# Layer 1 attention: three of four heads with held weights, one with moving weights

## The chip, the cores and the metric

The kernel runs on one core of one Trainium2 chip. The metric is the device time of one execution in microseconds (us); less is better. A core has five engines that run side by side and meet only at semaphores: TensorE (PE in the profile, with its loads of stationary operands as PEld), VectorE (DVE), ScalarE (ACT), GpSimd (POOL) and SyncE (SP). [...]

## The reference, cut to what matters

Two layers follow each other, each with a residual sum and a layer norm at its end. There are 16 graphs (batches) of 1024 nodes with 256 features and a 0/1 adjacency matrix for each. Layer 0 is graph attention with 4 heads of 64. The change is in the attention of layer 1, which has 8 heads of 32:

```python
normed = layer_norm(x, gamma1, beta1)
qkv = normed.reshape(b_, n_, H, HD).transpose(0, 2, 1, 3)
scale = 1.0 / jnp.sqrt(jnp.asarray(HD, dtype=x.dtype))
scores = jnp.einsum('bhqd,bhkd->bhqk', qkv, qkv) * scale
mask = adj_matrix[:, None, :, :] > 0
masked = jnp.where(mask, scores, -jnp.inf)
attn = jax.nn.softmax(masked, axis=-1)
out = jnp.einsum('bhqk,bhkd->bhqd', attn, qkv)
out = out.transpose(0, 2, 1, 3).reshape(b_, n_, d_)
x = x + out
y = layer_norm(x, gamma2, beta2)
mlp = jax.nn.gelu(y @ W1 + b1, approximate=False) @ W2 + b2
return x + mlp
```

Everything is float32. Queries, keys and values are the same tensor, so a block of weights comes out with keys on the partitions and queries along the free axis, which is what the product with the values needs.

## The kernel before

**Two layers at once.** While one batch is in layer 1, the next one or two are in layer 0. Both layers are generators (`layer0`, `layer1`) that emit a piece of work and yield. A planner at the end of `fast_path` picks which one emits next. It goes by two things: how much of its work a layer has done (fixed numbers handed over at each `yield`, 2.5 for a step of attention 1), held against a target course, and whether one layer would have to wait over 0.3 us longer than the other by the planner's own cost model (class `Pace`, which adds up a cost for each instruction on each engine). So instructions have a fixed order on each engine, written down when the program is built. Smaller follow-up work (dividing by sums, norms, transposes) is put into `chains`; `advance` emits the next part of a chain when the model says that its inputs are there.

**Attention 1** (`attention1`) goes over 32 steps in a batch: two halves of 512 queries (`n`), two groups of four heads (`quad`), eight blocks of 128 keys (`jb`); 512 steps in the whole run. A step has these parts:

- `exponentials`: four matmuls, one for each head, with 32 rows each on four row tiles of the array; then four ACT exponentials of 128x512 out of four PSUM banks (ring `ps`, four buffers, so all four banks are used by every step);
- `masked`, emitted one step later: two DVE multiplications of 128x1024 by the 0/1 mask, each over two heads;
- `products`, emitted three steps later (`LAG = 3`): weights times values, summed in PSUM over the eight blocks of keys.

**The two forms of product.** In both, the array is cut into four column tiles of 32, at output partitions 0, 32, 64 and 96. In the *moved* form the values (128x32) are held and the 512 weights of a head move past them; a second matmul with `unit` (a column of ones and 31 of zeros) gives the sums of the weights. Heads 0 and 1 go this way: four matmuls, one on each tile, with values of head 0, values of head 1, sums of head 0, sums of head 1. In the *held* form 32 queries' weights (128x32) are held and the 33 columns of values (the last is 1, so the sum comes with them) move. Heads 2 and 3 go this way: 2 heads x 4 blocks of queries x 4 tiles = 32 matmuls. The profile shows every float32 matmul as two loads and two matmuls, so a step has 8 of the moved form and 64 of the held form.

**Out of PSUM.** `moved` (512 columns) and `held` (264 columns) take the two buffers of the ring `po` and are used for the eight blocks of keys of a quad. Then `heads_out` runs, 64 times in the run: ACT copies `moved` to SBUF (`oT`, name `oT1`); DVE takes the reciprocal of the sums in `held` and multiplies; TensorE transposes `oT` with four 128x128 transposes into a bank `pt`; DVE divides again out of `pt`. The next quad can write to the two buffers only after the copy and the first division have read them. After the second quad `finish1` makes the residual and the norm, and `mlp` follows when all 32 steps are done.

In the profile every line is L61, the helper that records the instruction for the planner; groups are told apart by the names of tiles: `po<-p,v` and `po<-p,unit` are moved products, `po<-v,p` held ones, `ps<-nT` the logits of attention 1, `acc<-v,p` the products of layer 0, other `acc` lines layer 0's preparation and transposes, `ranges` and `o` the reciprocals and divisions of `heads_out`.

## Time and profile before

| | us |
|---|---|
| median of three runs | 3437.51 |
| lowest and highest run | 3434.63, 3438.09 |
| profiled execution, span from the first to the last instruction (the time that the profile gives for it) | 3453.7 |
| TensorE matmuls busy in the span | 3312.8 (96%) |
| DVE busy | 2981.3 (86%) |
| ACT busy | 1935.6 (56%) |
| mean granted TensorE clock | 0.980 of full |
| moved products, busy | 552.9 (values), 552.7 (sums), side by side |
| held products, busy | 391.4 |

The profiled execution is 16.2 us, 0.5%, above the median. Spans and waits in the text are from it. "Busy" is the time in which at least one instruction of a group is under way; the matmuls of a group overlap, so the mean duration of one (197 ns for a held one) says little, and the distance from one start to the next is what a matmul takes from the path. A batch takes some 210 us, the first half of it attention 1, the second half its MLP, both interleaved with layer 0 of a later batch.

### The profile page before, as it was taken

To read this page: it belongs to the slowest core of one execution; us is meant where nothing else is said; L and a number is where in the kernel's file an instruction comes from. 1 tells how busy PE (TensorE), PEld (TensorE's weight loads), DVE (VectorE), ACT (ScalarE), POOL (GpSimd) and SP (SyncE) were. 2 spreads that over 40 slices of the span, in tenths; PEclk is the share of its full clock that TensorE was granted. 3 is DMA by queue.
4 is the path that set the end of the run, shared out by engine and by line. 5 is a ranking of instruction groups with operands and counts; after the bars stand their busy time and mean duration, and the time that the engine had idled before them with its cause. 6 is when DMAs were issued, how large, how long until landed. Compare 5 with 4: busy or idle time off the path is not lost.

```text
span 3453.7 us, 141035 instructions
## 1 busy us (share of the span) xinstructions
PE 3312.8 (96%) x64161; PEld 2252.1 (65%) x64161; DVE 2981.3 (86%) x5262; ACT 1935.6 (56%) x4192; POOL 418.6 (12%) x424
## 2 busy tenths in 40 slices
PE   5899999999999999999999999999999999999998
PEld 4558576675856758576585766757667585775846
DVE  5898898988979898898988989889898898989883
ACT  2563846547375573746637466473654737556373
POOL 1102011010110101101020110101101011010200
PEclk9899999999999999999999999999999999999999
DMA  5211202011020111202112020120201102010000
GB/s 135 51 22 40 44 27 57 15 44 40 28 59 21 42 34 34 56 19 59 22 38 46 24 57 19 41 43 26 59 15 46 38 28 62 18 44 23 23 6 15
DMA packets 95728, 131.30 MB, mean 38 GB/s; under 512 B 10385, under 2 KB 61585, under 8 KB 95121
## 3 DMA queue, kind: packets, MB, share of 16 engines
q1 hardware_dynamic: 75104, 87.58, 8.2%
q0 software_dynamic: 18432, 33.56, 6.6%
q8 instruction: 504, 8.26, 1.0%
q10 hardware_dynamic: 1584, 1.05, 0.1%
q14 instruction: 104, 0.84, 0.1%
HBM read 138.68 MB, written 17.04 MB: 45 GB/s over the span
## 4 chain that ended last, share of the span: by engine, by line
PE 72%; DVE 20%; ACT 5%; issue 2%; DMA 1%; POOL 0%; SPq 0%; POOLq 0%; ACTq 0%; DVEq 0%
PE po L61 28%; PE ps L61 24%; PE acc L61 20%; DVE p L61 15%; ACT p L61 2%; DVE o L61 1%; DVE x L61 1%; ACT sq L61 1%; DVE st L61 1%; DVE z L61 1%; ACT mask L61 1%; ACT hb L61 1%; DVE v L61 0%; ACT z L61 0%; DVE hb L61 0%
## 5 line engine op out<-in xcount | busy, mean ns | idle before, releaser
L61 ACT ACTIVATE p<-ps 128x512 f32<-128x512 f32 x2006 | 1042.2, 616 | 384.1 <-PE ps L61 341.5
L61 DVE TENSOR_TENSOR p<-p,mask 128x1024 f32<-128x1024 f32 x1024 | 1186.6, 1217 | 6.8 <-ACT p L61 6.8
L61 DVE SCALAR_TENSOR_TENSOR p<-cb,dinv,mask 128x512 f32<-128x512 f32 x1024 | 711.0, 744 | 0.1
L61 ACT ACTIVATE hid<-ps,b_sb 128x256 f32<-128x256 f32 x512 | 242.0, 473 | 795.0 <-PE ps L61 794.7
L61 PE MATMUL ps<-nT 32*128 32x512 f32 x4012 | 676.3, 655 | 0.0
L61 PEld LDWEIGHTS po<-v,p 128*32 128x32 f32 x32768 | 396.1, 110 | 333.2 <-issue 288.5
L61 PE MATMUL acc<-v,p 128*64 128x65 f32 x16384 | 562.2, 226 | 31.0 <-DVE p L61 14.3
L61 PEld LDWEIGHTS acc<-v,p 128*64 128x64 f32 x16384 | 515.2, 140 | 112.9 <-issue 59.0
L61 PE MATMUL po<-p,v 128*32 128x512 f32 x2048 | 552.9, 615 | 0.0
L61 PE MATMUL po<-p,unit 128*32 128x512 f32 x2048 | 552.7, 615 | 0.0
L61 PE MATMUL ps<-yT,w_sb 128*128 128x256 f32 x2048 | 489.8, 385 | 0.0
L61 PE MATMUL po<-w_sb,hid 128*128 128x256 f32 x2048 | 474.6, 384 | 0.0
L61 PEld LDWEIGHTS po<-w_sb,hid 128*128 128x128 f32 x2048 | 381.7, 190 | 54.5
L61 PEld LDWEIGHTS ps<-yT,w_sb 128*128 128x128 f32 x2048 | 375.5, 190 | 51.5
L61 PE MATMUL po<-v,p 128*32 128x33 f32 x32768 | 391.4, 199 | 12.4 <-issue 8.5
L61 PEld LDWEIGHTS po<-p,v 128*32 128x32 f32 x2048 | 78.5, 109 | 332.9 <-issue 174.7
L61 PEld LDWEIGHTS ps<-nT 32*128 32x128 f32 x4012 | 220.1, 186 | 98.0 <-issue 41.3
L61 POOL TENSOR_TENSOR r<-v,mhalf 128x1 f32<-128x1 f32 (+1 forms) x192 | 157.6, 831 | 705.7 <-DVE v L61 623.8
L61 DVE TENSOR_TENSOR z<-acc,bias_r 128x256 f32<-128x256 f32 x128 | 54.1, 423 | 181.7 <-ACT hb L61 181.4
L61 PE MATMUL acc<-w0e,xT 128*128 128x264 f32 x512 | 154.1, 425 | 37.2 <-DVE z L61 22.9
L61 POOL DMA_DIRECT2D ak<-in_adj_dram x128 | 69.7, 545 | 971.5 <-PE acc L61 959.0
L61 POOL TENSOR_TENSOR r<-v1s,mhalf 128x4 f32<-128x4 f32 x32 | 61.5, 1922 | 981.1 <-DVE v1s L61 981.1
(111 smaller groups left out, 2818.5 us busy)
## 6 DMA issues: line engine op xcount, KB each, us to landing
ak<-in_adj_dram POOLq DMA_DIRECT2D x128, 256.0 KB, 3.9
cb<-esr SPq DMA_DIRECT2D x64, 512.0 KB
xk<-in_x_dram SPq DMA_DIRECT2D x64, 256.0 KB
xl<-in_x_dram SPq DMA_DIRECT2D x32, 512.0 KB
out_dram<-z SPq DMA_DIRECT2D x128, 128.0 KB
w_sb<-in_L_gnn_W_dram SPq DMA_DIRECT2D x2, 1024.0 KB
esr<-rows SPq DMA_DIRECT2D x64, 4.0 KB
v<-in_L_gnn_a_src_dram SPq DMA_DIRECT2D x2, 320.0 KB
```

The source lines that it names most:

```text
L61: return method(*args, **kwargs)
```

## The change

Of the four heads of a quad, head 0 alone has its weights moving. Its 512 queries are cut into two sides of 256, and the four column tiles take values of side 0, sums of side 0, values of side 1, sums of side 1: still four matmuls, of 256 columns each in place of 512. Heads 1, 2 and 3 have their weights held: 48 matmuls in place of 32. The moved ones still come first, then the held ones, head by head; head 1 takes its weights from the first pair's tile, heads 2 and 3 from the second's.

`moved` has 256 columns in place of 512, `held` 396 in place of 264. In `heads_out` the copy is 128x256, there are two transposes in place of four, the first division covers three heads (12 reciprocals and 384 products to a partition in place of 8 and 256), and the second covers one head in two parts, one for each side (2 reciprocals and 64 products each, in place of one with 8 and 256). The numbers handed to the planner at each yield and its course are not touched; its cost model sees the new instructions.

```diff
--- before.py
+++ after.py
@@ -218,6 +218,7 @@
     PAIR = 2
     GB = 2
     QUAD = 4
+    SIDE = HALF // 2
     NEAR0 = math.sqrt(0.5 - 2.0**-10)
     NEAR1 = math.sqrt(0.5 + 2.0**-10)
     SCALE1 = 1.0 / math.sqrt(HD)
@@ -761,22 +762,26 @@
 
         def products(quad, jb, ps, moved, held):
             values = half(jb // BPH)[1][:, jb % BPH, :, :]
-            for e in range(PAIR):
-                hd = quad * QUAD + e
-                for at, v in ((e, values[:, hd, 0:HD]), (PAIR + e, unit)):
+
+            for side in range(PAIR):
+                for i, v in enumerate((values[:, quad * QUAD, 0:HD], unit)):
+                    at = (side * PAIR + i) * Q
                     nc.tensor.matmul(
-                        moved[at * Q : (at + 1) * Q, :], v, ps[0][:, e, :], start=jb == 0, stop=jb == NB - 1
+                        moved[at : at + Q, :],
+                        v,
+                        ps[0][:, 0, side * SIDE : (side + 1) * SIDE],
+                        start=jb == 0,
+                        stop=jb == NB - 1,
                     )
-            for e in range(PAIR):
-                hd = quad * QUAD + PAIR + e
+            for e in range(1, QUAD):
                 for q in range(BPH):
                     for at in range(0, P, Q):
                         nc.tensor.matmul(
-                            held[at : at + Q, q, e, :],
-                            ps[1][:, e, q * P + at : q * P + at + Q],
-                            values[:, hd, :],
-                            start=jb == 0 and e == 0 and q == 0,
-                            stop=jb == NB - 1 and e == PAIR - 1 and q == BPH - 1,
+                            held[at : at + Q, q, e - 1, :],
+                            ps[e // PAIR][:, e % PAIR, q * P + at : q * P + at + Q],
+                            values[:, quad * QUAD + e, :],
+                            start=jb == 0 and e == 1 and q == 0,
+                            stop=jb == NB - 1 and e == QUAD - 1 and q == BPH - 1,
                         )
 
         LAG = 3
@@ -800,8 +805,8 @@
                 continue
             n, quad, jb = steps[i - LAG]
             if jb == 0:
-                moved = ps_o.tile([P, HALF], F32, name="po")
-                held = ps_o.tile([P, BPH, PAIR, HD + 1], F32, name="po")
+                moved = ps_o.tile([P, SIDE], F32, name="po")
+                held = ps_o.tile([P, BPH, QUAD - 1, HD + 1], F32, name="po")
             products(quad, jb, ready.pop(i - LAG), moved, held)
             if jb == NB - 1:
                 if quad == 0:
@@ -814,28 +819,34 @@
 
     def heads_out(n, quad, moved, held, o, rinv):
 
-        oT = two.tile([P, HALF], F32, name="oT1")
+        oT = two.tile([P, SIDE], F32, name="oT1")
         nc.scalar.copy(oT, moved)
         of_heads = o.rearrange("p k (h e) -> p k h e", e=HD)
         rinv = rinv[:, n * BPH : (n + 1) * BPH, :]
 
-        def divide(first, sums, src):
-            heads = slice(quad * QUAD + first, quad * QUAD + first + PAIR)
-            nc.vector.reciprocal(rinv[:, :, heads], sums)
+        yield "vector", held
+        heads = slice(quad * QUAD + 1, (quad + 1) * QUAD)
+        nc.vector.reciprocal(rinv[:, :, heads], held[:, :, :, HD])
+        nc.vector.tensor_mul(
+            of_heads[:, :, heads, :],
+            held[:, :, :, 0:HD],
+            rinv[:, :, heads][:, :, :, None].to_broadcast([P, BPH, QUAD - 1, HD]),
+        )
+        yield "tensor", oT, side_ready
+        pt = side_bank([P, SIDE // P, P])
+        for c in range(SIDE // P):
+            nc.tensor.transpose(pt[:, c, :], oT[:, c * P : (c + 1) * P], ident)
+        yield "vector", pt
+        hd = quad * QUAD
+        for side in range(PAIR):
+            mine = slice(side * SIDE // P, (side + 1) * SIDE // P)
+            sums = pt[:, :, (side * PAIR + 1) * Q]
+            nc.vector.reciprocal(rinv[:, mine, hd], sums)
             nc.vector.tensor_mul(
-                of_heads[:, :, heads, :], src, rinv[:, :, heads][:, :, :, None].to_broadcast([P, BPH, PAIR, HD])
+                of_heads[:, mine, hd, :],
+                pt[:, :, side * PAIR * Q : side * PAIR * Q + HD],
+                rinv[:, mine, hd][:, :, None].to_broadcast([P, SIDE // P, HD]),
             )
-
-        yield "vector", held
-        divide(PAIR, held[:, :, :, HD], held[:, :, :, 0:HD])
-        yield "tensor", oT, side_ready
-        pt = side_bank([P, BPH, QUAD, Q])
-        for q in range(BPH):
-            nc.tensor.transpose(
-                pt[:, q, :, :].rearrange("p e z -> p (e z)"), oT[:, q * P : (q + 1) * P], ident
-            )
-        yield "vector", pt
-        divide(0, pt[:, :, PAIR:, 0], pt[:, :, 0:PAIR, :])
 
     def finish1(o, x1, yT, heads):
```

## The prediction

> **What bounds the kernel now.** I read the page's busy times first, then the chain of waits, then the timeline of a few attention steps, then the stretches of one batch.

> ```profile
> span 3453.7 us, 141035 instructions
> PE 3312.8 (96%) x64161; PEld 2252.1 (65%) x64161; DVE 2981.3 (86%) x5262; ACT 1935.6 (56%) x4192; POOL 418.6 (12%) x424
> ...
> PE 72%; DVE 20%; ACT 5%; issue 2%; DMA 1%; POOL 0%; SPq 0%; POOLq 0%; ACTq 0%; DVEq 0%
> PE po L61 28%; PE ps L61 24%; PE acc L61 20%; DVE p L61 15%; ACT p L61 2%; DVE o L61 1%; DVE x L61 1%; ACT sq L61 1%; DVE st L61 1%; DVE z L61 1%; ACT mask L61 1%; ACT hb L61 1%; DVE v L61 0%; ACT z L61 0%; DVE hb L61 0%
> ```

> TensorE sets 72% of the end, but a fifth of the chain is DVE's, nearly all of it the mask multiplications. They take turns inside one batch, as the stretches of the batch from 1610 us show (busy time of PE, PEld, DVE, ACT, POOL; clock; DMA):

> ```profile
> 1625.00:1640.00 15.00, 14.92 (x369) 7.95 (x356) 11.30 (x15) 12.50 (x31) 0.53 (x1) 1.00 0.48 122
> 1640.00:1655.00 15.00, 15.00 (x356) 7.72 (x355) 12.56 (x15) 11.82 (x26) 1.06 (x2) 1.00 0.20 39
> ...
> 1685.00:1700.00 15.00, 14.74 (x446) 8.06 (x440) 14.93 (x19) 10.45 (x21) 0.00 (x0) 1.00 0.01 3
> 1700.00:1715.00 15.00, 15.00 (x478) 8.53 (x474) 14.93 (x18) 6.26 (x13) 0.00 (x0) 1.00 0.01 3
> ```

> In the first half of attention 1 DVE has 2.4 to 3.7 us in 15 to spare; in the last 45 us none. The chain of waits there says the same: TensorE step by step, then one run of DVE.

> ```profile
> 1623.61 1.56 PE po L61 x69
> 1625.17 1.09 PE acc L61 x4
> 1626.25 1.07 PE ps L61 x8
> 1627.33 1.56 PE po L61 x69
> ...
> 1697.91 11.72 DVE p L61 x12
> ```

> The products' price is in the timeline (start, duration), in two steps that follow each other without a change of array shape between:

> ```profile
> 1708.59 0.62 PE L61 MATMUL po<-p,v 128*32 128x512 f32 x1
> ...
> 1709.05 0.59 PE L61 MATMUL po<-p,v 128*32 128x512 f32 x1
> ...
> 1709.47 0.73 PE L61 MATMUL po<-v,p 128*32 128x33 f32 x63
> 1710.01 0.60 PE L61 MATMUL po<-p,v 128*32 128x512 f32 x1
> ...
> 1710.87 0.76 PE L61 MATMUL po<-v,p 128*32 128x33 f32 x64
> 1711.56 0.63 PE L61 MATMUL acc<-v,p 128*64 128x65 f32 x14
> ```

> Start to start, the moved products take 0.88 us in two passes (0.46 and 0.42), the 64 held ones 0.54 (8.4 ns each) or 0.68 where the array's shape changes after them. A step's products are 1.56 us, as in the chain.

> **The change, part by part.**

> *Moved products.* The same eight instructions pass 256 columns in place of 512. Column time halves: of 0.883 us, 0.854 is two passes of 0.427, so -0.427 us a step. Bounds: 0 if a pass has a floor, -0.44 if the start halves too. I take -0.427, because 256 columns on the whole array (po<-w_sb,hid) go by in 3.65/16 = 0.228 us a pass, against 0.427 for 512.

> *Held products.* 32 instructions more (16 matmuls of two passes): 32 x 8.4 ns = +0.268 us a step. Bounds: 32 x 8.4 below, and above 32 x 30.7 ns = 0.98 (layer 0's held products, 2.949 us for 96). I take 8.4: same tile, same columns, and 64 in a row show no slowing.

> Net -0.159 us a step, -81.4 us over 512 steps if every step were on the path.

> [...]

> *How much is on the path.* From the chain of waits, window by window over the run, 292 runs of products (19 hold two steps', so 311 of 512 steps) lie on it with most of their time. What a step on the chain gives back depends on the logits' four banks. After a short step the fourth logit waits for the fourth exponential of the step before:

> ```profile
> 1703.18 1.77 PE L61 MATMUL ps<-nT 32*128 32x512 f32 x8
> 1703.83 0.29 PEld L61 LDWEIGHTS ps<-nT 32*128 32x128 f32 x2 [0.20 <-ACT p L61]
> ```

> The step from logits at 1700.55 to logits at 1703.18 took 2.63 us, and these logits 1.70 start to start instead of 1.07. From logits to exponentials 1.16 us and four exponentials 2.06 make a loop of 3.22 us; a step shorter than that hands its gain to a longer wait in the next. Steps on the chain by length: 147 over 3.374 us give 0.159 each, 23.4 us; 18 between 3.215 and 3.374 give what they exceed the loop by, 2.4; 75 below give nothing, and 11.9 us stay out. 44 steps' products at the tails, after the batch's last logits, give 7.0. In the last batch, where no layer 0 is left and six banks take turns, the chain's 30 steps give 4.8. Sum -37.6 us.

> *Two transposes fewer* (four took 0.585 into acc, 0.49 into ps; 0.27 for two): 36 of 64 sets are on the chain, -9.7 us. *The copy to oT* falls from 0.60 to 0.41 (COPY hb<-acc, 128x256, 410 ns): -0.19 at 18 places, -3.5. Elsewhere it stands ahead of the next exponentials on ACT, which has 44% free.

> *Divisions.* Reciprocal to product takes 0.235 us, product to the next instruction 0.342. Three heads: 8 to 12 elements adds 0.025 (177 ns for 4, 202 for 8) and 256 to 384 adds 0.13 (424 ns for 256, 684 for 512), +0.155. Two sides: twice about 0.20 + 0.15 in place of 0.577, +0.12. So +0.275 for each heads_out, 17.6 us in all. [...] 48 of 128 divisions are on the chain: +6.6 us.

> *Held products alone on the chain* (17 places, where the moved ones were already past): 17 x 0.268 = +4.6 us. No DMA is issued in a changed step. *Clock:* after PE had idled 2.6 us, at 3314 us, a pass took 0.61 in place of 0.42; no wait that grows here comes near that, so I take nothing for it (above: as many such places more, 3 us each).

> Sum: -37.6 - 9.7 - 3.5 + 6.6 + 4.6 = -39.6 us. It is a ceiling of sorts: the chain names only the last releaser, and others stood close behind. In six of the batches DVE's run starts some 15 steps in, in the others five steps later, so the two engines are nearly level there. Bounds are 0 (all absorbed) and -39.6; I take 60%, as DVE has a fifth of its time free in the stretches where most of the gain is made: -24 us. On the median, 3437.5 - 23.5 = 3414 us; in the profiled execution 3430.

> **The rivals.**

> *Absorbed.* DVE or the exponentials set every step, and PE just waits longer. For: 75 chain steps already at the loop, DVE full for 45 us a batch. Against: 147 long steps with no stall. 3437 us, or 3431 to 3444.

> *The order falls worse (slower).* The planner's model sees cheaper products too, and what it takes as late decides which layer emits next. Place: two attention steps with no layer 0 work between. The run has 94 such bare steps before the last batch; the one above took 2.63 us, and the next logits stood 0.63 longer. After the change it would be 2.47 us, and 3.215 - 2.47 = 0.745 is lost at each. A fifth of them (DVE's share of the chain) would cost nothing, so 40 more bare steps, two and a half a batch, use up the 24 us; 72 more cost 72 x 0.8 x 0.745 = 43 us: 3457. Against: a step hands the planner the same amount of work done as before.

> *Held products slow down in longer runs (slower).* If the added 32 cost twice the row, 16.8 ns (an estimate between 8.4 and 30.7), a step loses 0.11 us instead of gaining: 311 x 0.11 = +34, with the -9.7, -3.5 and +6.6 above 3465 us. The break-even is 0.427/32 = 13.3 ns for each added one. Against: every run of 64 goes at 8.4.

> *Everything kept.* All 81 us, the transposes' 128 x 0.135 = 17, less the divisions' 18: 3357 us, if the steps on DVE's runs gained as well. Against: DVE busy 14.93 of 15 there.

> **How the numbers follow.** Forecast (3390 to 3430) 0.50; everything kept 0.08; absorbed 0.14; order worse 0.21; held slower 0.07. Faster by over 0.2% (7 us, about what a measurement here can tell from none): 0.58; within: 0.14; slower: 0.28. For 8 in 10 I leave out the deep part of "kept" (0.06) and the dear ends of the two slower ones (0.13): 3380 to 3466; the forecast's own range is 3390 to 3430.

> **What would show it.** Moved products at 0.46 us and 96 held ones in 0.80 (0.94 with a change of shape) confirm the prices. More time in fourth-logit waits on ACT and in PE's waits for DVE p, by about 12 us and up, shows where the lost part went. DVE's busy time should rise by some 18 us, PE's fall by 40 to 90. I am wrong if a held matmul takes 10 ns or more, if bare steps grow well beyond 94, or if the chain turns to DVE for more than 30%.

## The result and the profile after

The changed kernel takes 3596.45 us (median of four runs, 3585.14 to 3599.10) against 3437.80 us before: 1.0442 times as long, with a 95% interval of 1.0416 to 1.0467 (the ratios here are those on record; the quotient of the two medians is 1.0461). By the medians it is 158.7 us slower where 23.5 us less was forecast, and it lies far outside the range of 3380 to 3466.

The page of the changed kernel gives the same views as before: span, busy times, one group of products, the instruction queue.

```profile
span 3594.6 us, 173690 instructions
PE 3299.6 (92%) x80417; PEld 2428.2 (68%) x80417; DVE 2999.4 (83%) x5390; ACT 1920.0 (53%) x4192; POOL 414.6 (12%) x424
q8 instruction: 631, 10.34, 1.2%
L61 PE MATMUL po<-v,p 128*32 128x33 f32 x49152 | 578.1, 199 | 165.0 <-issue 155.5
```

The last line's second field is the idle time of TensorE just before the group, and what ended it. The same two lines of the kernel before, which the prediction does not use:

```profile
q8 instruction: 504, 8.26, 1.0%
L61 PE MATMUL po<-v,p 128*32 128x33 f32 x32768 | 391.4, 199 | 12.4 <-issue 8.5 <-DVE o L61 3.3
```

TensorE's share fell from 96% to 92% of a longer span. It did not get more work (busy 3312.8 before, 3299.6 after). It stands idle in front of held products for 165.0 us where it stood 12.4, and nearly all of that is "issue": no semaphore, engine or transfer that the profile shows released it. The chain of waits of the changed kernel reaches back only to 3066 us, over the last 15% of the span, so it is no help here.

The timeline of TensorE in the changed kernel (start, duration; in brackets the idle time before) shows what the idle time looks like:

```profile
1919.89 0.88 PE L61 MATMUL po<-v,p 128*32 128x33 f32 x80
1920.94 0.33 PE L61 MATMUL po<-v,p 128*32 128x33 f32 x16 [0.17 <-issue]
1921.20 1.16 PE L61 MATMUL acc<-w0e,xT 128*128 128x264 f32 x4
1922.29 1.14 PE L61 MATMUL ps<-nT 32*128 32x512 f32 x8
1923.36 0.44 PE L61 MATMUL acc<-ident,oT 128*128 128x128 f32 x2
1923.73 0.40 PE L61 MATMUL po<-p,v 128*32 128x256 f32 x1
...
1923.97 0.38 PE L61 MATMUL po<-p,v 128*32 128x256 f32 x1
...
1924.19 0.95 PE L61 MATMUL po<-v,p 128*32 128x33 f32 x89
1926.72 0.27 PE L61 MATMUL po<-v,p 128*32 128x33 f32 x7 [1.59 <-issue]
1926.91 0.71 PE L61 MATMUL ps<-nT 32*128 32x512 f32 x4
```

The moved products cost what was forecast: first pass at 1923.73, second at 1923.97, held ones from 1924.19, so 0.46 us. But a run of 96 held ones stops in the middle: after 80 in one step, after 89 in the next. Between the two stops lie 16 held matmuls, 4 of layer 0, 8 logits, 2 transposes, 8 moved, 89 held: 127 matmuls, each with its load, so 254 instructions and two waits on semaphores, 256 in all.

With that the step's arithmetic is another one. A bare attention step before has 80 matmuls, 160 instructions, in 2.63 us: 256 in 4.2 us. After the change it has 112, 224 instructions, in 2.47 us: 256 in 2.8 us, which the loop stretches to 3.5. With a unit of layer 0's products (32 matmuls in 1.08 us) it is 4.2 before and 3.2 after.

### The profile page after: what moved, and what is told of

Read it like the earlier page. It is cut to its first block, busy times and chain, and to the rows that moved or that the text cites. A ratio compares the mean times of both kernels' runs of the same rounds, so it can differ in the third digit from the quotient of the medians.

```text
span 3594.6 us, 173690 instructions
## 1 busy us (share of the span) xinstructions
PE 3299.6 (92%) x80417; PEld 2428.2 (68%) x80417; DVE 2999.4 (83%) x5390; ACT 1920.0 (53%) x4192; POOL 414.6 (12%) x424
## 5 line engine op out<-in xcount | busy, mean ns | idle before, releaser
L61 ACT ACTIVATE p<-ps 128x512 f32<-128x512 f32 x2006 | 1042.4, 615 | 436.5 <-PE ps L61 393.6
L61 DVE TENSOR_TENSOR p<-p,mask 128x1024 f32<-128x1024 f32 x1024 | 1188.2, 1218 | 20.1 <-ACT p L61 19.4
L61 PEld LDWEIGHTS po<-v,p 128*32 128x32 f32 x49152 | 561.5, 111 | 278.2 <-issue 192.5
L61 PE MATMUL po<-v,p 128*32 128x33 f32 x49152 | 578.1, 199 | 165.0 <-issue 155.5
L61 DVE SCALAR_TENSOR_TENSOR p<-cb,dinv,mask 128x512 f32<-128x512 f32 x1024 | 709.7, 744 | 0.0
L61 PE MATMUL ps<-nT 32*128 32x512 f32 x4012 | 699.0, 665 | 2.2 <-issue 2.2
L61 ACT ACTIVATE hid<-ps,b_sb 128x256 f32<-128x256 f32 x512 | 239.1, 473 | 844.7 <-PE ps L61 844.4
L61 PE MATMUL acc<-v,p 128*64 128x65 f32 x16384 | 567.9, 227 | 35.1 <-issue 10.4
L61 PEld LDWEIGHTS acc<-v,p 128*64 128x64 f32 x16384 | 520.1, 141 | 117.2 <-issue 60.6
L61 PE MATMUL ps<-yT,w_sb 128*128 128x256 f32 x2048 | 484.6, 386 | 1.5 <-issue 1.5
L61 PE MATMUL po<-w_sb,hid 128*128 128x256 f32 x2048 | 473.0, 383 | 0.0
L61 PEld LDWEIGHTS ps<-yT,w_sb 128*128 128x128 f32 x2048 | 381.9, 191 | 55.8 <-issue 2.1
L61 PEld LDWEIGHTS po<-w_sb,hid 128*128 128x128 f32 x2048 | 381.8, 190 | 53.4
L61 PE MATMUL po<-p,unit 128*32 128x256 f32 x2048 | 332.3, 399 | 1.2 <-issue 1.2
L61 PE MATMUL po<-p,v 128*32 128x256 f32 x2048 | 331.9, 399 | 0.1
L61 PEld LDWEIGHTS po<-p,v 128*32 128x32 f32 x2048 | 78.8, 109 | 345.6 <-issue 199.0
L61 PEld LDWEIGHTS ps<-nT 32*128 32x128 f32 x4012 | 230.1, 189 | 109.6 <-issue 44.2
L61 POOL TENSOR_TENSOR r<-v,mhalf 128x1 f32<-128x1 f32 (+1 forms) x192 | 153.6, 810 | 688.1 <-DVE v L61 605.3
L61 DVE TENSOR_TENSOR z<-acc,bias_r 128x256 f32<-128x256 f32 x128 | 54.2, 423 | 202.0 <-ACT hb L61 199.9
L61 PE MATMUL acc<-w0e,xT 128*128 128x264 f32 x512 | 157.0, 432 | 36.7 <-DVE z L61 22.9
L61 POOL TENSOR_TENSOR r<-v1s,mhalf 128x4 f32<-128x4 f32 x32 | 61.5, 1923 | 1091.3 <-DVE v1s L61 1091.3
L61 POOL DMA_DIRECT2D ak<-in_adj_dram x128 | 69.7, 545 | 1002.3 <-PE acc L61 988.8
```

Of the source, the lines that this page charges most:

```text
L61: return method(*args, **kwargs)
```

## Experiments

Two theories besides that of the instructions were open: that the planner, which saw cheaper products, had put the work into a worse order, and that a held matmul is dearer in runs of 96. All ratios are to the kernel before, run alongside on the same chip (medians 3450.51 us in the first four experiments, 3448.91 in the last two).

### The changed work in the old order

```diff
+            for e in range(PAIR):
+                for v in (values[:, quad * QUAD + e, 0:HD], unit):
+                    nc.enter("tensor", "matmul", (Told(moved, Q, HALF), v, ps[0][:, e, :]), {})
+            for _ in range(PAIR * BPH * P // Q):
+                nc.enter("tensor", "matmul", (Told(held, Q, HD + 1), ps[1][:, 0, 0:Q], values[:, 0, :]), {})
+            nc.deaf = True
             for side in range(PAIR):
...
+            nc.deaf = False
```

`nc.enter` books an instruction with the planner without issuing it; while `deaf` is set, what is issued is not booked. `heads_out` is told the old copy, transposes and divisions in the same way.

> The changed kernel's instructions in exactly the order of the kernel before: the planner is told before's matmuls, copies and divisions while the changed ones are issued. Instruction theory (TensorE's instructions come in 16 KB packets of 256, and 256 of them never take less than about 3.4 us; the 96 held products of a step empty the packet faster, and 202 us of stalls inside held runs are the loss): as slow as the changed kernel, 3570 to 3620 us, stalls inside held runs 170 to 230 us. Order theory (the planner placed the work worse once it saw cheaper products; bare steps rose from 94 to 108): the loss goes, 3400 to 3440 us.

3626.00 us, 1.0520 times (1.0501 to 1.0538). The held runs' distances over 0.06 us come to 223.4 us. In the old order the changed work is slower by 175.5 us, in its own by 158.7: the planner's new order is not the loss.

### The old work in the new order

The mirror: the products and `heads_out` of before, while the planner is told the changed ones.

```diff
+            for _ in range(PAIR):
+                for v in (values[:, quad * QUAD, 0:HD], unit):
+                    nc.enter("tensor", "matmul", (Told(moved, Q, SIDE), v, ps[0][:, 0, 0:SIDE]), {})
...
+            nc.deaf = True
             for e in range(PAIR):
                 hd = quad * QUAD + e
...
```

> The mirror of the run in the old order: the instructions of the kernel before in exactly the changed kernel's order (the planner is told the changed ones). Instruction theory: as fast as before but for 14 more bare steps at about 0.6 us, 3430 to 3465 us, stalls inside held runs under 30 us. Order theory: about 3570 to 3600 us.

3455.23 us, 1.0015 times (0.9999 to 1.0031); 8.8 us in held runs. The two groups of held products, first of the changed work in the old order, then of the old work in the new one (L64 is the same helper, three lines further down):

```profile
L64 PE MATMUL po<-v,p 128*32 128x33 f32 x49152 | 583.1, 199 | 179.9 <-issue 172.0
```

```profile
L64 PE MATMUL po<-v,p 128*32 128x33 f32 x32768 | 390.5, 198 | 8.2 <-issue 4.6
```

The idle time goes with the instructions and not with the order. For the old work the order is worth 0.15%, 0.31% at the interval's end.

### One head's held products left out

```diff
             for e in range(1, QUAD):
+                nc.mute = e == QUAD - 1 and jb > 0
                 for q in range(BPH):
                     for at in range(0, P, Q):
                         nc.tensor.matmul(
                             held[at : at + Q, q, e - 1, :],
-                            ps[e // PAIR][:, e % PAIR, q * P + at : q * P + at + Q],
+                            ones if e == QUAD - 1 else ps[e // PAIR][:, e % PAIR, q * P + at : q * P + at + Q],
...
```

`mute` books the matmul and does not issue it. The planner sees the constant in place of the last head's weights, so a few steps come in another order than in the changed kernel.

> The changed kernel in its own order, but the held products of the quad's last head are left out in seven of eight key blocks (in the first block a constant stands in for its weights), so a step has 64 held instructions as before and TensorE has 14 of 512 x 0.268 us less. Instruction theory: the 202 us of stalls fall under 30 and about 70 us of work on the path go as well, 3300 to 3390 us. Order theory, or a higher price of each held matmul: only the work goes, 120 us at most, 3470 to 3540 us.

3406.28 us, 0.9877 times (0.9854 to 0.9900): 44 us faster than before, where the changed kernel is 159 slower. Of these 203 us the work that was left out accounts for 120 at 8.4 ns a matmul; the stops in held runs fell from 203.5 us to 58.0. Against a dearer matmul this run alone says little, as the work left out would then be worth more than 120 us. The changed kernel itself settles that: of 483 runs of 96 held matmuls that nothing interrupts, 258 have no stop inside, and these go at 8.6 ns a matmul in the median.

The run missed the instruction theory's 3300 to 3390 as well. 58.0 us were left in held runs where under 30 were expected: 44.9 at packet boundaries, nearly all the rest waits for DVE's masks. Its page has 34.7 us of "issue" in front of held products, against 155.5 in the changed kernel:

```profile
L64 PE MATMUL po<-v,p 128*32 128x33 f32 x32768 | 406.0, 199 | 67.3 <-issue 34.7
```

That stops remain at all fits the numbers: the moved products had become shorter and an undisturbed bare step of 160 instructions now takes 2.2 us, 256 in 3.5, just at the loop.

### 64 queries held at a time

```diff
             for e in range(1, QUAD):
                 for q in range(BPH):
-                    for at in range(0, P, Q):
+                    for at in range(0, P, TILE):
                         nc.tensor.matmul(
-                            held[at : at + Q, q, e - 1, :],
-                            ps[e // PAIR][:, e % PAIR, q * P + at : q * P + at + Q],
+                            held[at : at + TILE, q, e - 1, :],
+                            ps[e // PAIR][:, e % PAIR, q * P + at : q * P + at + TILE],
...
```

> The changed kernel with the weights held 64 queries at a time on two column tiles, in place of 32 on four: 48 held instructions in a step for the same arithmetic. Instruction theory: stalls inside held runs under 15 us; if each costs about 15.6 ns (half of layer 0's 30.7 ns for 65 columns) 3370 to 3430 us; if the load of 64 columns bounds each at 27 to 31 ns, a step's held products take 1.3 to 1.5 us and the time is 3520 to 3650 us, still without stalls. Order theory: 3570 us or more, with held runs at 0.75 us.

3650.88 us, 1.0588 times (1.0569 to 1.0607): the dearer of the two branches. From the page of this kernel:

```profile
span 3650.8 us, 124523 instructions
PE 3535.5 (97%) x55841; PEld 2586.1 (71%) x55841; DVE 2999.5 (82%) x5390; ACT 1924.4 (53%) x4192; POOL 418.7 (11%) x424
q8 instruction: 439, 7.19, 0.8%
L61 PE MATMUL po<-v,p 128*64 128x33 f32 x24576 | 829.3, 226 | 0.0
```

With fewer instructions the idle time in front of held products is 0.0 and TensorE is back at 97%: the stalls are gone, with the same three heads held and as many bare steps as in the changed kernel (108). The time is lost elsewhere: 48 held matmuls take 1.42 us, 29.6 ns each, where the array's shape stays the same after them, though they move 33 columns where layer 0's move 65 for 30.7; and the moved products ahead of them take 0.57 us in place of 0.46. So the time goes with the 64 columns that are held and not with the columns that move; whether their load sets it was not shown.

### The price of 256 instructions by itself

```diff
     while chains:
         run(chains[0])
+    for i in range(2048):
+        if i % 16 == 0:
+            spare = ps_s.tile([P, BPH, HD + 1], F32, name="ps")
+        at, q = i % 4 * Q, i // 4 % BPH
+        nc.nc.tensor.matmul(spare[at : at + Q, q, :], unit, g1_r[:, 0 : HD + 1], start=True, stop=True)
```

> The kernel before with a run of 2048 extra held matmuls (4096 instructions pairs of load and matmul, 128x32 by 33 columns, on the four column tiles in turn, of constants, never read) after the last of TensorE's work; the planner is not told of them. It measures the disputed price by itself. 8192 instructions are 32 packets of 256. Instruction theory: 32 x 3.4 to 3.5 us = 109 to 112 us on the time, and the run stalls once in 256 instructions. A price for each matmul alone (8.4 ns for each pass): 4096 x 8.4 ns = 34 us.

3565.52 us, 116.6 us more than before (1.0338 times, 1.0317 to 1.0359): 3.6 us for each packet, where the matmuls' own 8.4 ns would have made 34 us of it. The timeline of TensorE at the end of this kernel:

```profile
3430.12 2.65 PE L1048 MATMUL ps<-g_r,unit 128*32 128x33 f32 x268
3434.97 1.38 PE L1048 MATMUL ps<-g_r,unit 128*32 128x33 f32 x128 [2.20 <-issue]
3438.99 1.99 PE L1048 MATMUL ps<-g_r,unit 128*32 128x33 f32 x128 [2.65 <-issue]
3442.47 1.99 PE L1048 MATMUL ps<-g_r,unit 128*32 128x33 f32 x128 [1.49 <-issue]
3446.22 1.99 PE L1048 MATMUL ps<-g_r,unit 128*32 128x33 f32 x128 [1.76 <-issue]
```

Exactly 128 matmuls with their loads, then a wait, 29 times in a row (the first five rows are shown). From one start to the next it is 3.47, 3.75 or 4.02 us, 3.73 on average (108.1 us for 29), with no other engine at work and 2% of the DMA engines in use, so this is not contention with other transfers.

### All four heads held

```diff
-            for e in range(PAIR):
-                hd = quad * QUAD + e
-                for at, v in ((e, values[:, hd, 0:HD]), (PAIR + e, unit)):
-                    nc.tensor.matmul(
-                        moved[at * Q : (at + 1) * Q, :], v, ps[0][:, e, :], start=jb == 0, stop=jb == NB - 1
-                    )
-            for e in range(PAIR):
-                hd = quad * QUAD + PAIR + e
+            for e in range(QUAD):
                 for q in range(BPH):
                     for at in range(0, P, Q):
                         nc.tensor.matmul(
-                            held[at : at + Q, q, e, :],
-                            ps[1][:, e, q * P + at : q * P + at + Q],
+                            held[e // PAIR][at : at + Q, q, e % PAIR, :],
+                            ps[e // PAIR][:, e % PAIR, q * P + at : q * P + at + Q],
...
```

`heads_out` then has no copy and no transposes, and both divisions read PSUM.

> All four heads with their weights held, 32 queries at a time (two PSUM tiles of 264 columns, no moved products, no sums by unit, no copy to oT, no transposes, all divisions straight out of PSUM). By the price of each instruction a step's products take 128 x 8.4 ns + 0.14 = 1.21 us against 1.56 before, so without the instruction theory it is faster than before: 3320 to 3400 us. Instruction theory: a bare step has 272 instructions, 272/256 x 3.5 = 3.7 us against 2.63 before, one with a unit of layer 0's products 336/256 x 3.5 = 4.6 against 3.7; stalls inside held runs over 400 us and 3650 to 3780 us.

3911.41 us, 1.1331 times (1.1303 to 1.1360). By the instructions' own prices this is the cheapest of all the forms, and it is the slowest by far. The direction is the instruction theory's, and so is the size in the held runs (483.1 us), but the total is 130 us above its range. From the page, then the granted clock of this run:

```profile
q8 instruction: 726, 11.89, 1.3%
L61 PE MATMUL po<-v,p 128*32 128x33 f32 x65536 | 802.5, 204 | 393.8 <-issue 391.3
L61 PE MATMUL ps<-nT 32*128 32x512 f32 x4012 | 718.0, 686 | 29.3 <-issue 25.3
L61 PE MATMUL acc<-v,p 128*64 128x65 f32 x16384 | 586.8, 230 | 60.3 <-issue 40.7
```

```profile
core 0: 3910.0 us, clock 0.943
```

Three things were left out of the expectation. The stops are not confined to held products: 57 more stand at packet boundaries in other work, above all in logits and layer 0's products, with 92 us of idle time (6 and 1.6 us in the kernel before). The loop of a packet is nearer 3.7 us than 3.5: 3.75 in the median of the 426 times that TensorE waits at two boundaries in a row. And TensorE's clock is at half for longer: the trace's clock records have 25 spells of half clock, 143.5 us together, in the kernel before, 40 and 203.7 us in the changed kernel, 80 and 444.1 us here, against 24 and 176.3 us in the run with 64 queries held at a time, which has no such stops. What part of the 130 us each makes up was not separated; nor was the planner's order, which is another one here.

## Why the prediction was wrong

**What failed** is the step *Held products*: "I take 8.4: same tile, same columns, and 64 in a row show no slowing." 8.4 ns is right for a matmul whose instructions are there, and 96 of them do take 0.943 us with the change of shape where nothing stops them. But held runs took 1.37 us on average against 0.71 before, because they now outrun the instruction packets. In the sum the stops are 203.5 - 12.3 = 191 us that no term held. The upper bound of that step, 30.7 ns for each added instruction or 0.98 us a step, would have covered it: the added 32 cost 1.37 - 0.71 = 0.66 us. The rival "held products slow down in longer runs" came nearest, with a break-even of 13.3 ns for each added one where 0.66/32 = 21 were measured, but with a price of 16.8 and a chance of 0.07. It counted the price of an instruction and not the instructions: the page's 504 packets of 16 KB, and 19 stops in held runs at "issue", stood in the profile of before.

"64 in a row show no slowing" is true of the 64 and did not carry over to a longer stream: the run of nothing but such matmuls goes at 3.73 us for 128, 29 ns each. The matmul itself did not become dearer: in the changed kernel's runs without a stop a held one takes 8.6 ns.

**What held.** The moved products fell to 0.456 us as worked out. DVE's busy time rose by 18.1 us (2981.3 to 2999.4) against 17.6 from the divisions' sizes. Transposes went from 0.585 and 0.49 to 0.367 and 0.275 us, 0.22 less a set and not 0.27. TensorE's busy time fell by 13 us, not by 40 to 90, perhaps in part because a busy matmul at half clock is longer (in the changed kernel layer 0's products stand 54 ns apart in the spells of half clock, 30 ns elsewhere); no run separates this.

**The rest of the sum.** The stops in held runs grew by 191 us, more than the whole 158.7. Stops at packet boundaries in TensorE's other work come to 25 us (27 of them), against 3 before (6), measured as distances over the usual ones. That leaves 158.7 - 191 - 22 = -54 us for everything else, the order included; the changed work in the old order gives 175.5 - 211 - 23 = -59 in the same way. The prediction's sum of terms was -39.6, of which it took 60%. So either the cheaper products, transposes and copies returned more than that whole sum, or some of the stops were not on the path; no run separates the two, and the extra spells of half clock are on neither side.

**The other rivals.** *The order falls worse*: bare steps rose, from 94 to about 108, and the two runs with exchanged orders show that this doesn't matter at this size. *Absorbed*: DVE was not the limit. Here are two stretches of a batch of the changed kernel, from its first and its last part of attention 1, with the columns as before:

```profile
1922.00:1937.00 15.00, 13.41 (x469) 8.10 (x468) 10.77 (x17) 10.49 (x27) 0.53 (x1) 1.00 0.26 47
1982.00:1997.00 15.00, 13.34 (x546) 8.91 (x550) 14.86 (x23) 8.21 (x17) 0.00 (x0) 1.00 0.02 4
```

In the first, no engine is full: TensorE 13.41 of 15 us, DVE 10.77, ACT 10.49; the others wait for TensorE, and TensorE for instructions (its idle 1.59 us are the one stop ahead of 1926.72). In the last part DVE still is full.

**Clock.** "No wait that grows here comes near that": waits of up to 3.4 us appeared, and the half-clock spells rose from 25 to 40.

No run here beat the kernel before with the whole computation. The form with two heads moved sits where it does for a reason that the prices of single instructions don't show: 256 instructions in 4.2 us, against a loop of 3.5 to 3.75.

## What to carry to other kernels

TensorE's stream had a budget of instructions here as well as one of time: in the run of small matmuls 256 of them, 128 float32 passes with their loads, took 3.47 to 4.02 us, 3.73 on average, and in the changed kernel no packet began more than one ahead, so that a slow stretch saved up little for a dense one (11 of 13 stopped all the same). Before large matmuls are traded for many small ones, divide the instructions of the densest 256 by their time; "issue" as the releaser inside a run of like instructions, at a distance of 256, was the sign of it here. The price from a short burst was a lower bound for a longer one: 8.4 ns in a row of 64, 29 ns in the long run.

## What the runs showed that was not expected

- The instruction packets: in the changed kernel's held runs every stop of over 0.25 us is at the same place of 256 instructions, ended 1.39 us after a packet of 1.0 us; 3.73 us for 256 with nothing else running.
- Held matmuls of 33 columns on 64-wide tiles take 29.6 ns each, about as long as layer 0's with 65 columns (30.7), while on 32-wide tiles they take 8.4.
- In the kernels with more stops TensorE's clock was lower: 0.980 of full on average before, 0.972 in the changed kernel, 0.943 with four heads held, and 0.51 in the run of small matmuls, where 128 of them take 1.74 us from the first start to the last in place of 1.07. Stops are not all that lowers it: with 64 queries held at a time there are none, and it is 0.976.
